# A vision tower on one core: one attention product moved by a group, and the row gathers of a linear-attention layer started in sixes

## The chip, the cores and the metric

The program runs on one core of a Trainium2 chip. The core has five engines with queues of their own: TensorE (PE) for matrix products, VectorE (DVE), ScalarE (ACT), GpSimd (POOL) and SyncE (SP), which issues most transfers. The metric is the device time of one execution in microseconds. Before the change it is 721.51 us, the median of three runs (718.78, 721.51 and 723.24).

## The reference

Everything is float32. The reference is a tokenizer for four images and two transformer layers. Tokens of one image are repeated three times, so the kernel computes 784 rows an image and writes each row out three times. The parts that the change touches are the first attention and the second one:

```python
# layer 0: attention between the images, one weight for a pair of images and a channel of a head
att = einsum('slhc,tlhc->sth', q, k) * scale     # sum over rows l and channels c
att = softmax(att, axis=1)
o = einsum('sth,tlhc->slhc', att, v) * g
...
# layer 0: a mixture of six experts, two for each row
combined = sum(sel * routing_weights[..., None], axis=2)
...
# layer 1: linear attention
q, k, v = split(layernorm(h) @ W_qkv + b_qkv, 3, axis=2)
q2 = _l2_normalize(q*q / (sum(q*q) + EPS_DIV), axis=-1)      # q and k have their means taken off
k2 = _l2_normalize(k*k / (sum(k*k) + EPS_DIV), axis=-2)
kv = einsum('bnc,bnd->bcd', k2, v)
attn = v + einsum('bnc,bcd->bnd', q2, kv) / sqrt(N)
h = h + attn @ W_out + b_out
```

In the first attention a "product" is one entry of `einsum('slhc,tlhc->sth')` before the sum over a head's channels: image s times image t, summed over the 784 rows, for one half of the 256 channels. In the mixture the two expert results of a row lie in HBM wherever the routing put them, so the second layer has to gather them row by row.

## The kernel before

**Layout.** The rows of the residual stream `h` are held in 25 tiles of 128 rows by 256 channels: six tiles an image, and one (`LT`) for the sixteen rows that each image has left over. The program is unrolled: every loop below is a Python loop that emits instructions.

**Front.** The tiles are worked in eight `groups` of three, the first with the left-over tile added. `keys_values(g)` takes the normalised, transposed rows of group g and computes its part of K and V on PE; ACT copies the results into `kT` and `vT`. In between it does three things for later groups: `second_norm(g + 2)`, the statistics of group g+2, which alternate between DVE (means and variances, reciprocals) and ACT (square roots); `turn_second(g + 1)`, transposes on PE and their ACT copies into `mT`, from which the next group's products are taken; and on DVE `second_rows(g + 2)`, and the addition of a bias to `h`. The order is written out by hand for PE, ACT and DVE, so an engine takes its instructions in exactly the order in which the code calls them.

After group 1 the queries of image 0 are computed. Then, after each odd group, DVE takes two products of image 0, one for each half `o` of the channels, with the image whose keys have just been finished: `products(0, o, [g // 2])`. Each is one DVE instruction over 128 x 784 elements, with its sum read out after it. The products with the last image follow behind the loop.

**Experts.** Rows are scattered to HBM by expert (`send`, one indirect DMA from POOL for each tile and choice), PE works the blocks, and results go back to `yrows` in HBM.

**Layer 1, linear attention.** The 24 full tiles are `units` 0 to 7 of three tiles each, and the left-over tile is unit 8 (`LU`). For one unit the steps are

- `fetch(u)`: for each of its three tiles and both choices one indirect DMA on POOL's queue that gathers 128 rows of 1 KB from `yrows` into the tile `ys`: six gathers for a unit, in the order (tile 0, choice 0), (tile 0, choice 1), (tile 1, choice 0) and so on. `ys` has three buffers, so unit u reuses the buffer of unit u-3 and waits until that was read.
- `stats_one(u, j)`: DVE adds the two gathered tiles to `h`, weighted, and takes mean and variance of tile j. These two additions (line 1760) are the only readers of `ys`.
- `norm_root(u)`, `norm_rows(u)` (together `normalise`): square root on ACT, then DVE writes the normalised rows to `xa`, one of four tiles used in turn (`xa_of(u)`).
- `x_t(u)`: transposes on PE, copied by ACT or DVE into `lxT`; `qk_mm`, `qk_add`, `qk_squares`: queries and keys; `scales(u)` and `fold(u)`: their norms.
- For each image b: `k_x_tiles`, `k_x_left` (the products of keys and rows, PE), `k_norm(b)` (PE sums the squared keys into `pn`, ACT takes the root into `kn`, DVE the reciprocal), `k_x_out` (DVE scales the products by `kn` into `g`), `g_t` (PE transposes `g`, ACT copies), `kv_out` (PE and DVE), and then `rows_out` for its two units.

The part up to `rows_out(1)` is written out by hand for PE, ACT, DVE and POOL. Behind it a loop `for u in range(4, LU + 2)` leaves the order to the scheduler of the framework. The calls of `fetch` stand in this order: units 0, 1, LU and 2 among the expert blocks; 3 and 4 one after the other behind the four POOL instructions that mask the left-over rows (`xaM`, line 2222); 5 and 6 later in the hand-written part; 7 at the top of the loop's first pass. Since POOL has nothing else to do there, its queue holds the thirty gathers of units 3 to 7 one after the other, held back only by the three buffers.

Of the kernel before, what the change touches and what calls it, by code (L numbers as in the profile page):

```python
# [21 lines left out]
F32 = mybir.dt.float32  # L22
# [50 lines left out]
def tile_vit_tower(ctx: ExitStack, tc: tile.TileContext, a: dict, out: bass.AP):  # L73
    nc = tc.nc
# [267 lines left out]
    groups = [list(range(g, g + 3)) for g in range(0, NT - 1, 3)]  # L342
# [1020 lines left out]
    with tc.manual_schedule(engines=by_hand):  # L1363
        last_rows(n - 2)
        turn_second(0)
        second_rows(1, second_norm(1))
        keys_values(0)
        for g in range(1, len(groups)):
            keys_values(g)

            if g == 1:
                for o in range(2):
                    q_mm(0, o)
                    q_copy(0, o)
            if g % 2 and g + 1 < len(groups):
                for o in range(2):
                    products(0, o, [g // 2])
    front.close()
# [196 lines left out]
    past, u, ua, ub = (s - 2, 0, TPI), (s - 1, 0, TPI), (s, 0, GT), (s, GT, TPI + 1 - GT)  # L1575
# [137 lines left out]
    LU = len(units)  # L1713
# [10 lines left out]
    def xa_of(u):  # L1724
        return xaL if u == LU else xas[u % 4]

    def own_of(pool, u, shape, tag, bufs):
        if u == LU:
            return pool.tile([shape[0], 1, *shape[2:]], F32, tag=f"{tag}L", name=tag, bufs=1)
        return pool.tile(shape, F32, tag=tag, name=tag, bufs=bufs)  # L1730

    xaM = lina.tile([TT, NI, D + 2], F32, tag="xaM", name="xaM", bufs=1)
    for xa in (*xas, xaL):
        nc.gpsimd.memset(xa[:, :, D : D + 2], 1.0)
    xTs, qTs, uks, qks, sums, gs, kvos, stats, ys = ({} for _ in range(9))

    def fetch(u):

        if u >= len(units):
            return  # L1740
        b, j0, n = units[u]
        y = ys[u] = own_of(lina, u, [TT, UT, 2, D], "ys", 3)
        for j in range(n):
            for k in range(2):
                t = b * TPI + j0 + j
                got = nc.gpsimd.indirect_dma_start(  # L1746
                    out=y[:, j, k, :], out_offset=None, in_=yrows[:, :],
                    in_offset=bass.IndirectOffsetOnAxis(ap=pos[:, k, t : t + 1], axis=0),
                )
                tc.add_to_no_dep_group("fetched", got.ins)  # L1750

    lw, behind = [], []
# [27 lines left out]
    def normalise(u):  # L1780
        norm_root(u)
        norm_rows(u)
# [10 lines left out]
    def norm_rows(u):  # L1793
        if u >= len(units):
            return
        b, j0, n = units[u]
        t0 = b * TPI + j0
        mv, r = stats.pop(u)
        nc.vector.reciprocal(r[:, :n], r[:, :n])
        xa = xa_of(u)  # L1800
        for j in range(n):
            nc.vector.tensor_scalar(
                xa[:, j, :D], h[:, t0 + j, :], mv[:, j, 0:1], r[:, j : j + 1],
                ALU.subtract, ALU.mult,
            )
        if len(pending) < 7:
            pending.append(u)
        else:
            residual(u)
# [248 lines left out]
    def scales(u):  # L2058
        root(u)
        factors(u)  # L2060
        k_rows(u)
        q_rows(u)
        return k_squares(u)
# [41 lines left out]
    def k_norm(b):  # L2105

        acc = sums.pop(b)
        pn = psum_s.tile([P, 512], F32, tag="pss", name="pn")
        for c in range(2):
            of_c = slice(c * P, (c + 1) * P)  # L2110
            nc.tensor.matmul(pn[:, c : c + 1], acc[:, of_c], ones[:TT], start=True, stop=False)
            nc.tensor.matmul(
                pn[:, c : c + 1], squares[LU][:, 0, of_c], ofimage[:, b : b + 1],
                start=False, stop=True,
            )
        kn = small.tile([P, 2], F32, tag="kn", name="kn")
        nc.scalar.activation(kn, pn[:, :2], AF.Sqrt, scale=float(REP), bias=zero)
        nc.vector.tensor_scalar(kn, kn, 1e-12, None, ALU.max)
        nc.vector.reciprocal(kn, kn)
        return kn  # L2120

    def k_x_out(b, kn):
        g = gs[b] = lin.tile([P, 2, D + 2], F32, tag="g", name="g")
        for c in range(2):
            nc.vector.tensor_scalar(
                g[:, c, :], pgxs.pop((b, c)), kn[:, c : c + 1], REP / math.sqrt(REP * SEQ),
                ALU.mult, ALU.mult,
            )
# [32 lines left out]
    def rows_out(u):  # L2161
        for done in rows_out_parts(u):
            pass
        return done
# [39 lines left out]
    with tc.manual_schedule(engines=by_hand | {ENG.Pool}):  # L2204
        x_t(1)
        for j in range(UT):
            qk_mm(0, j)
            qk_add(0, j)
            qk_squares(0, j)
        root(0)  # L2210
        for j in range(UT):
            qk_mm(1, j)
        qk_add(1, 0)
        qk_squares(1, 0)
        stats_one(LU, 0)
        norm_root(LU)
        factors(0)
        qk_add(1, 1)
        qk_squares(1, 1)
        norm_rows(LU)  # L2220
        for b in range(NI):
            nc.gpsimd.tensor_scalar(
                xaM[:, b, :], xaL[:, 0, : D + 2], ofimage[:, b : b + 1], None, ALU.mult
            )
        fetch(3)
        fetch(4)
        qk_add(1, 2)
        qk_squares(1, 2)
        root(1)
        q_rows(0)  # L2230
        stats_one(2, 0)
        next(steps)
        x_t(LU)
        q_t(0)
        k_rows(0)
        next(steps)
        stats_one(2, 1)
        factors(1)
        q_rows(1)
        k_rows(1)  # L2240
        qk_mm(LU, 0)
        stats_one(2, 2)
        norm_root(2)
        next(steps)
        Wvo, bvo = lw[:2]
        q_t(1)
        qk_add(LU, 0)
        qk_squares(LU, 0)
        root(LU)
        norm_rows(2)  # L2250
        fetch(5)
        squares[0] = k_squares(0)
        factors(LU)
        fold(0, squares.pop(0))
        k_rows(LU)
        squares[LU] = k_squares(LU)
        q_rows(LU)
        squares[1] = k_squares(1)
        fold(1, squares.pop(1))
        k_x_tiles(0)  # L2260
        x_t(2)
        k_x_left(0)
        kn = k_norm(0)
        k_x_out(0, kn)
        qk_mm(2, 0)
        qk_add(2, 0)
        qk_squares(2, 0)
        stats_one(3, 0)
        qk_mm(2, 1)
        qk_add(2, 1)  # L2270
        qk_squares(2, 1)
        q_t(LU)
        gT = g_t(0)
        stats_one(3, 1)
        qk_mm(2, 2)
        qk_add(2, 2)
        kv_out(0, gT)
        qk_squares(2, 2)
        stats_one(3, 2)
        normalise(3)  # L2280
        rows_out(0)
        x_t(3)
        root(2)
        factors(2)
        k_rows(2)
        q_rows(2)
        fetch(6)
        for j in range(2):
            qk_mm(3, j)
            qk_add(3, j)  # L2290
            qk_squares(3, j)
            stats_one(4, j)
        squares[2] = k_squares(2)
        qk_mm(3, 2)
        qk_add(3, 2)
        qk_squares(3, 2)
        stats_one(4, 2)
        root(3)
        norm_root(4)
        norm_rows(4)  # L2300
        parts_ = rows_out_parts(1)
        next(parts_)
        fold(2, squares.pop(2))
        factors(3)
        k_rows(3)
        q_t(2)
        x_t(4)
        for done in parts_:
            pass
        q_rows(3)  # L2310
        squares[3] = k_squares(3)
        fold(3, squares.pop(3))
        behind.append(done.ins.name)
    one_side[0] = False
    later = {5: (0, 1), 6: (2, 3), 7: (4, 5, 6)}
    for u in range(4, LU + 2):
        b, odd = divmod(u - 2, 2)
        one_image = not odd
        if u + 3 < LU:
            fetch(u + 3)  # L2320
        if u == LU:
            shared = shared1(0)
        if one_image:
            k_x(b)
            q_t(u - 1)
        if u < LU:
            q_k(u, 0, 2)
        if one_image:
            gT = g_t(b)
        if u < LU:  # L2330
            q_k(u, 2, UT)
            squares[u] = scales(u)
        if one_image:
            kv_out(b, gT)
        if u == LU - 1:
            rows_in(0)
            turn_rows(0)
            gate(0)
        if u < LU - 1:
            x_t(u + 1)  # L2340
        done = rows_out(u - 2)
        for k in later.get(u, ()):
            residual(pending[k], done.ins.name)
        if u == LU + 1:
            rows_left()
        if u < LU:
            fold(u, squares.pop(u))
            if u % 2:
                q_t(u - 1)
# [103 lines left out]
```

## Time and profile before

| what | us |
|---|---|
| median of three runs | 721.51 |
| the profiled execution's own time | 743.29 |
| its span, first to last instruction | 741.6 |
| PE busy in the span | 692.4 |
| DVE busy | 459.2 |
| ACT busy | 331.7 |
| POOL busy | 127.2 |

The profiled execution is 21.8 us longer than the median. Its stages, from the view that cuts the span into windows:

| stage (us from the start) | length | PE busy | POOL busy | granted PE clock |
|---|---|---|---|---|
| tokenizer, 0 to 130 | 130 | 120.27 | 18.77 | 1.00 |
| keys, values, attention, 130 to 207 | 77 | 73.20 | 0.00 | 0.98 |
| attention and the row scatters, 207 to 303 | 96 | 84.12 | 54.81 | 0.93 |
| experts, 303 to 434 | 131 | 128.69 | 12.79 | 1.00 |
| linear attention begins, 434 to 462 | 28 | 24.84 | 17.85 | 1.00 |
| 462 to 480 | 18 | 7.67 | 11.42 | 0.83 |
| linear attention, 480 to 600 | 120 | 117.67 | 11.52 | 0.98 |
| last mixture, 600 to 742 | 142 | 135.98 | 0.00 | 0.99 |

A line of the timeline reads: start, busy time, engine, line of the code, operation, out<-in, shapes, and how many instructions are merged into it. In square brackets stands how long the engine was idle before it and what released it. "issue" means that the profile shows no wait, and "remote" or "another core or an unknown queue" that it found no event near enough to name. The end of a PE instruction is modelled, not observed.

### The profile page before, as it was taken

The numbers are of one execution on the slowest core, as the hardware profiler recorded it, in microseconds if no ns is written. First come the engines' busy times: TensorE is split into PE (matmuls) and PEld (weight loads), VectorE is DVE, ScalarE is ACT, GpSimd is POOL, SyncE is SP. The second block draws the span as 40 slices with busy tenths as digits, with TensorE's granted clock in tenths as the row PEclk, the third lists the DMA queues.
The fourth block names the chain that finished last, engine by engine and source line by source line (L and its number), as shares of the span: only waits on it lengthen the run. The fifth ranks groups of instructions, "written<-read, shape, count | busy, mean of one in ns | idle before, by whom it ended". The sixth has DMA issues, their size and how long they took to land.

```text
span 741.6 us, 9843 instructions
## 1 busy us (share of the span) xinstructions
PE 692.4 (93%) x3043; PEld 477.3 (64%) x3043; DVE 459.2 (62%) x1385; ACT 331.7 (45%) x816; POOL 127.2 (17%) x238
## 2 busy tenths in 40 slices
PE   7899999899998897999999998499999999999996
PEld 4556655566655686788888856267776855555553
DVE  6476865769988643357555668179978653444441
ACT  1565674556797652223322337154645232222221
POOL 6300000000065356200002328533000000000000
PEclk9999999999999898999999999799999999999999
DMA  6999997000036834222334432211000013321333
GB/s 192 334 426 425 426 425 300 0 1 0 1 121 193 290 103 140 92 86 93 94 114 128 147 97 79 85 43 42 2 1 1 4 29 118 108 87 52 121 106 100
DMA packets 56476, 96.49 MB, mean 130 GB/s; under 512 B 6696, under 2 KB 46350, under 8 KB 56424
## 3 DMA queue, kind: packets, MB, share of 16 engines
q1 hardware_dynamic: 49924, 79.69, 30.1%
q0 software_dynamic: 5600, 14.32, 6.3%
q10 hardware_dynamic: 900, 1.86, 0.8%
q8 instruction: 24, 0.39, 0.2%
q14 instruction: 28, 0.23, 0.1%
HBM read 30.75 MB, written 65.09 MB: 129 GB/s over the span
## 4 chain that ended last, share of the span: by engine, by line
PE 55%; DVE 5%; ACT 2%; another core or an unknown queue 2%; issue 1%; DMA 1%; SPq 0%; DVEq 0%; ACTq 0%
PE pb L1539 13%; PE pe L320 6%; PE pyb L1557 6%; PE ps L320 5%; PE pqk L1994 4%; PE ps L2403 3%; PE pout L2173 3%; PE pout L2178 3%; PE pukx L2093 2%; PE pt L311 2%; PE pe L2373 2%; PE ps L2397 2%; PE ptb L1524 1%; PE pkvo L2153 1%
## 5 line engine op out<-in xcount | busy, mean ns | idle before, releaser
L1154 POOL DMA_INDIRECT xrows<-xn,pos x50 | 54.2, 1084 | 217.9 <-DVE nm L1010 178.3
L1746 POOL DMA_INDIRECT ys<-yrows,pos x50 | 49.2, 984 | 151.4 <-DMA yrows<-yb 120.0
L1545 ACT ACTIVATE hb<-pb,own 128x256 f32<-128x256 f32 (+1 forms) x74 | 33.5, 457 | 57.2 <-PE pb L1539 33.1
L1539 PE MATMUL pb<-xTb,own 128*128 128x256 f32 (+1 forms) x240 | 53.3, 364 | 4.8 <-ACT xTb L1528 2.6
L1539 PE MATMUL pb<-hb,own 128*128 128x256 f32 (+1 forms) x240 | 54.6, 368 | 0.3 <-DVE hb L1547 0.2
L1557 PE MATMUL pyb<-own,hb 128*128 128x256 f32 x216 | 53.5, 388 | 0.3 <-ACT hb L1545 0.2
L1994 PE MATMUL pqk<-Wqkv,lxT 128*128 128x512 f32 x100 | 47.7, 624 | 3.4 <-issue 3.2
L1539 PEld LDWEIGHTS pb<-xTb,own 128*128 128x128 f32 x240 | 42.1, 191 | 10.6 <-ACT xTb L1528 3.2
L320 PE MATMUL pe<-xT,eW 128*128 128x512 f32 (+1 forms) x112 | 46.0, 553 | 0.0
L1557 PEld LDWEIGHTS pyb<-own,hb 128*128 128x128 f32 x216 | 41.1, 195 | 6.8 <-ACT hb L1545 1.1
L1539 PEld LDWEIGHTS pb<-hb,own 128*128 128x128 f32 x240 | 41.9, 195 | 5.1 <-DVE hb L1547 0.9
L1563 DVE TENSOR_TENSOR yb<-pyb,eb 128x512 f32<-128x512 f32 (+1 forms) x30 | 19.1, 638 | 37.7 <-PE pyb L1557 32.8
L637 PE MATMUL pw<-Wall,pT 128*128 128x512 f32 (+1 forms) x96 | 42.4, 592 | 0.0
L1528 ACT COPY xTb<-ptb 128x512 f32<-128x512 f32 (+1 forms) x30 | 16.3, 542 | 54.4 <-PE ptb L1524 46.2
L907 DVE SCALAR_TENSOR_TENSOR prod<-kq 128x784 f32<-128x784 f32 x32 | 30.6, 970 | 13.2 <-issue 5.9
L1994 PEld LDWEIGHTS pqk<-Wqkv,lxT 128*128 128x128 f32 x100 | 19.4, 202 | 24.0 <-issue 22.1
L320 PEld LDWEIGHTS pe<-xT,eW 128*128 128x128 f32 x112 | 20.2, 190 | 21.6 <-issue 16.5
L1515 DVE COPY own<-kq 128x1540 f32 x30 | 29.1, 974 | 6.6 <-ACT xTb L1528 3.1
L311 PEld LDWEIGHTS pt<-ident,xn 128*128 128x128 f32 x200 | 24.3, 145 | 12.7 <-issue 10.0
L1547 DVE TENSOR_SCALAR hb<-pb,own 128x256 f32<-128x256 f32 (+1 forms) x46 | 20.3, 445 | 17.9 <-PE pb L1539 17.4
L637 PEld LDWEIGHTS pw<-Wall,pT 128*128 128x128 f32 (+1 forms) x96 | 17.9, 189 | 20.5 <-issue 18.5
L311 PE MATMUL pt<-ident,xn 128*128 128x128 f32 x200 | 29.0, 284 | 1.8 <-issue 1.6
(418 smaller groups left out, 1439.7 us busy)
## 6 DMA issues: line engine op xcount, KB each, us to landing
xrows<-nothing SPq DMA_DIRECT2D x22, 896.0 KB
yrows<-nothing SPq DMA_DIRECT2D x22, 896.0 KB
out_dram<-h SPq DMA_DIRECT2D x23, 384.0 KB
xb<-xrows SPq DMA_DIRECT2D x24, 256.0 KB
yrows<-yb SPq DMA_DIRECT2D x24, 256.0 KB
kq<-in_L_ffn_expert_w_dram SPq DMA_DIRECT2D x18, 256.0 KB
wb<-wd SPq DMA_DIRECT2D x16, 128.0 KB
img<-in_x_dram SPq DMA_DIRECT2D x5, 294.0 KB
```

Source lines behind the costliest of these rows:

```text
L311: nc.tensor.transpose(pt[:, j * TT : (j + 1) * TT], xn[:, j, c * P : (c + 1) * P], ident[:TT, :TT])
L320: nc.tensor.matmul(pm[: wcols.stop - wcols.start, :n], w[:, c, wcols], xT(c), start=(c == 0), stop=(c == chunks - 1),)
L637: nc.tensor.matmul(pm, pixels(c, tiles[j]), Wall[: K1[c], c, :], start=(c == 0), stop=(c == 1))
L907: nc.vector.scalar_tensor_tensor(prod, qTs[s][:, o, :], 1.0, kT[:, o, t * SEQ : (t + 1) * SEQ], ALU.mult, ALU.mult, accum_out=atts[s][:, o ...
L1154: put = nc.gpsimd.indirect_dma_start(out=xrows[:, :], out_offset=bass.IndirectOffsetOnAxis(ap=pos[:, k, t0 + j : t0 + j + 1], axis=0), in_ ...
L1515: nc.vector.tensor_copy(w, ewf[0][:, bass.ds(off, EW)])
L1539: nc.tensor.matmul(pm, wm[:, c, o * P : (o + 1) * P], src[:, c, :], start=(c == 0), stop=(c == 1),)
L1545: nc.scalar.activation(dst[:, o, :], pm, AF.Relu, bias=b)
L1557: nc.tensor.matmul(pm[:, t, :], src[:, c, t * P : (t + 1) * P], wm[:, c, :], start=(c == 0), stop=(c == 1),)
L1746: got = nc.gpsimd.indirect_dma_start(out=y[:, j, k, :], out_offset=None, in_=yrows[:, :], in_offset=bass.IndirectOffsetOnAxis(ap=pos[:, k, ...
L1994: nc.tensor.matmul(pqk, xTs[u][:, c, cut(j, 1)], Wqkv[:, c, : 2 * D], start=(c == 0), stop=(c == 1),)
L2173: nc.tensor.matmul(pm[:, i, :], xT[:, c, cut(j, 1)], Wvo[:, c, :], start=(c == 0), stop=False,)
```

## The change

In the front, the product of image 0 with itself for the second half of the channels is taken after group 2 instead of after group 1. The later products stay: the third branch catches groups 3 and 5 as before.

In the linear attention, `fetch` gets a second argument, one element of a tile. When it is given, POOL first copies that element into a new one-element tile `paused`; the gathers are called after it. The fetches are moved in the code: unit 4's from behind `xaM` to behind the reciprocal of image 0's norm (`kn`), unit 5's to behind unit 3's normalised rows, unit 6's to behind unit 4's, and unit 7's to the end of the loop's first pass, with an element of unit 5's rows.

```diff
@@ the front
-            if g % 2 and g + 1 < len(groups):
+            if g == 1:
+                products(0, 0, [0])
+            elif g == 2:
+                products(0, 1, [0])
+            elif g % 2 and g + 1 < len(groups):
                 for o in range(2):
                     products(0, o, [g // 2])
@@ the tiles of the linear attention
     xaM = lina.tile([TT, NI, D + 2], F32, tag="xaM", name="xaM", bufs=1)
+    paused = lina.tile([1, 1], F32, tag="paused", name="paused", bufs=1)
...
-    def fetch(u):
+    def fetch(u, behind=None):
 
         if u >= len(units):
             return
         b, j0, n = units[u]
+        if behind is not None:
+            nc.gpsimd.tensor_copy(paused, behind)
         y = ys[u] = own_of(lina, u, [TT, UT, 2, D], "ys", 3)
@@ the part written out by hand
         fetch(3)
-        fetch(4)
         qk_add(1, 2)
...
         norm_rows(2)
-        fetch(5)
         squares[0] = k_squares(0)
...
         k_x_left(0)
         kn = k_norm(0)
+        fetch(4, kn[:1, :1])
         k_x_out(0, kn)
...
         normalise(3)
+        fetch(5, xa_of(3)[:1, 0, :1])
         rows_out(0)
...
         q_rows(2)
-        fetch(6)
...
         norm_rows(4)
+        fetch(6, xa_of(4)[:1, 0, :1])
         parts_ = rows_out_parts(1)
@@ the loop
     for u in range(4, LU + 2):
         b, odd = divmod(u - 2, 2)
         one_image = not odd
-        if u + 3 < LU:
-            fetch(u + 3)
...
         if u < LU:
             q_k(u, 2, UT)
             squares[u] = scales(u)
+            if u + 3 < LU:
+                fetch(u + 3, xa_of(u + 1)[:1, 0, :1])
```

Built, the two kernels have the same instructions in the same order on PE, ACT and SP. DVE's order differs by the one product. POOL's queue behind `xaM` is, before, thirty gathers; after, six gathers, the copy of `kn`, six gathers, the copy of unit 3's element, six gathers, the copy of unit 4's element, twelve gathers, the copy of unit 5's element.

## The prediction, made before the changed kernel ran

> **What bounds the kernel now.** I read the page first, then the windows by stage, the chain of waits in order of time, and the timelines of single engines around each moved instruction.
>
> ```profile
> span 741.6 us, 9843 instructions
> PE   7899999899998897999999998499999999999996
> PE 55%; DVE 5%; ACT 2%; another core or an unknown queue 2%; issue 1%; DMA 1%; SPq 0%; DVEq 0%; ACTq 0%
> ```
>
> PE is the bound nearly everywhere. One slice in forty stands out, with 4 tenths. The windows place it: between 462 and 480 us PE is busy 7.67 of 18 us, while POOL issues gathers without a pause. The chain of waits, in order of time, has two pieces there that belong to no engine:
>
> ```profile
> 460.99 1.34 ACT sq L2055 x4
> 462.33 4.61 another core or an unknown queue
> 466.97 0.48 ACT lxT L94
> 467.44 0.95 issue
> 468.39 0.48 ACT lxT L94
> 468.87 10.05 another core or an unknown queue
> 478.95 0.27 ACT kn L2117
> ```
>
> The timelines of PE, ACT, DVE and POOL say who waits for whom:
>
> ```profile
> 463.98 0.36 PE L2112 MATMUL pn<-ofimage,sq 128*128 128x1 f32 x2
> ...
> 478.95 0.26 ACT L2117 ACTIVATE kn<-pn,zero 128x2 f32<-128x2 f32 x1 [10.07 <-remote]
> ...
> 479.24 0.17 DVE L2118 TENSOR_SCALAR kn<-kn 128x2 f32<-128x2 f32 x1 [16.01 <-ACT kn L2117]
> ...
> 475.83 0.94 POOL L1746 DMA_INDIRECT ys<-yrows,pos  x1 [0.30 <-issue]
> ```
>
> ACT's root needs only `pn`, whose last matmul stands at 463.98, with a modelled end of 464.34. It starts 14.6 us later, 2.2 us after the last of eighteen gathers issued without a wait (454.14 to 476.77). DVE waits for that root and PE for DVE. The waits show a smaller case in the row scatters, POOL's other indirect DMAs:
>
> ```profile
> DVE sel L1144 <- remote: 6.9, 1, 6.9
> ACT hb L1545 <- remote: 5.3, 1, 5.3
> ```
>
> There `pcount` ends at 274.93 by its model and DVE takes it at 281.02, 1.1 us after a run of twelve scatters (264.63 to 279.89). So in this execution PE's results arrive late when POOL has issued many indirect DMAs in a row. I call it the hold-up; its price here is 478.95 less the 464.5 at which `kn` could have run, 14.4 us.
>
> **The change part by part.**
>
> *The product.* In front of group 2's statistics ACT and PE wait:
>
> ```profile
> 143.97 0.30 ACT L286 ACTIVATE rstd<-mv,eps 128x3 f32<-128x3 f32 x1 [1.18 <-DVE mv L284]
> 145.81 2.85 PE L320 MATMUL pkv<-mT,Wk 128*128 128x384 f32 x8 [0.30 <-ACT mT L1317]
> ```
>
> One product is 0.89 us from start to start (140.45, 141.35, 142.24). Without the second one DVE's statistics begin at 141.35 and ACT's root 0.89 us sooner, inside its wait of 1.18. PE gets back at most its 0.30. Behind group 2's addition, which now ends 0.89 earlier, the product takes the 0.89 again, so group 3's statistics start at 147.56 as before. ACT's next root (149.28) has no wait in front, its copies `mT` run from 150.42 to 151.63, and PE wants the second of them at about 151.8 even when 0.3 sooner. The product's result is first read at 162.71. Sum: -0.3 us; bounds 0 and -0.3 (with a gain of 0.89 excluded by PE's own wait).
>
> *The gathers.* Nothing is removed: thirty gathers stay, 0.95 us each and 0.30 between, 1.25 apart; six take 7.5. From the start of a gather to the landing of its rows is 2.5 to 2.8 us (501.86 to 504.4, 508.18 to 511.0). POOL's queue holds nothing else behind them, and SP's is not touched. Every fetch is on the path only if its first reader on DVE has to wait:
> - Unit 4 starts after `kn` (reciprocal ends at 479.61): rows from 482.4, all by 488.7; DVE wants them at 496.26, 498.42 and 500.59. Slack over 11 us.
> - Unit 5 starts after the first row of unit 3 (ends 490.66): rows from 493.4 to 499.7; wanted from 507.50 to 512.41. Slack over 11.
> - Unit 6 starts after the first row of unit 4 (ends 503.26): rows from 506.0, every 1.25 us to 512.3; the readers stand at 511.27, 512.89, 515.32, 516.59, 518.86, 520.31. Slack 5.2 at the least.
> - Unit 7 has no pause: its copy stands behind its gathers in POOL's queue, since the loop is left to the scheduler and nothing ties them. It follows unit 6 at 510.9: rows from 513.5; wanted at 519.34, 522.79 and from 527.80. Slack 5.8.
>
> All four slacks lie behind `kn`, so they stay if the hold-up before it goes. Cost 0; the cover is those microseconds, and what is late beyond them is paid one for one, as the weighted additions stand in DVE's order ahead of `kn` of image 1 (512.33), for which PE waits.
>
> *Four copies of one element on POOL.* No such row is in the trace; the nearest are POOL's memsets of one column, 0.10 us, and its 128x258 rows, 1.02. I take 0.2 each; either end fits into 5.2. A gain is excluded for work that is added.
>
> *Waits.* DVE's rows of unit 7 and ACT's root of image 3 now name POOL, whose copies were done some 40 us and more before: 0. The table load ahead of that last root now waits for PE's `pn`. It ran at 577.20, when `pn` was just done, and DVE used `kn` only at 583.05, 3.6 us after it was ready (579.49). Cost 0, the cover 3.6.
>
> *The hold-up.* With the change POOL stops at 461.5 until `kn` is there, so in an execution like this one `pn` would come at about 463.6 to 464.5 and 13 to 14.4 us go. A new hold-up may come from the twelve gathers of units 6 and 7 (503.4 to 518.5): the twelve scatters cost 6.1.
>
> Does the timed kernel pay the hold-up at all? The timed median is 21.8 us below this execution. PE is idle 49.6 us in the windows of all stages, and its instructions run at one rate wherever it is fed (0.43 us for 512 columns), so the 21.8 must come out of idle time or a lower clock. If the 14.4 stayed, the other 39 us, mostly the first transfers (9.7), the tail (6.0) and short dependencies, would have to give 21.8. If it goes, and with it the late results beside the scatters (2.7 us of PE before 281.28, 1.9 before 294.90, some colder clock), the sum is about 20. So I take the hold-up as belonging mostly to the profiled execution: -0.3 for the timed kernel, not -14.
>
> Two rules of the Trainium skill bear on this. The rows say PE's results are 14.4 us late beside gathers. "SBUF — State Buffer", section Who interferes with whom, says a DMA never contends with a compute engine and only VectorE and GpSimd share a port: by it spacing the gathers is worth nothing, 721.2; by the row alone, 707. "NOTIFIC — the notification-queue block", section 7.1, says that the recorder's internal pipeline holds its producers back rather than lose a record. No row here shows that, but it would reconcile the two and agrees with the idle-time count.
>
> Sums: the profiled execution, 743.29 - 0.3 - 13 or so, plus 0 to 6: 730 to 736. The timed one, 721.51 - 0.3 = 721.2.
>
> **The rivals.**
> - *The hold-up is real in timed runs.* For: it is in the rows, and twice beside POOL. Against: the idle-time count. Then 721.5 - 13.2 + 0 to 6 gives 708 to 714.
> - *The hold-up moves onto the twelve gathers, slower than before.* Before, units 6 and 7 were two sixes with a pause of 5.4 us (496.48 to 501.86); after, they are twelve in a row beside `k_x(1)`, where PE has no idle time to lose. If timed runs feel this and not the place at 464, the price is 6.1 as for the twelve scatters, and about 1.7 for PE's colder clock afterwards (four matmuls at 0.85 instead of 0.43 us from 467.50): 721.2 + 7.8 = 729. It decides once unit 6's and 7's gathers hold up PE by more than their surroundings absorb. Against: the sixes now there (489.26, 501.86) held nothing up on the chain.
> - *The change doesn't do what it says.* It is so for unit 7, whose rows aren't paused. If POOL's copies held nothing else either, 721.2 as well.
>
> **How the numbers follow.** About 1% (7.2 us: 714.3 and 728.7) is what a measurement of this kernel tells from no change. Likeliest, 0.81: nothing on the path but -0.3, 721.2, between 718 and 725 as the three runs spread. Hold-up real: 0.14, 708 to 714.3 in 0.12 of it. Moved onto the twelve: 0.04. Rows late by more than 5.2 us for another reason: 0.01. So faster 0.12, within 1% 0.83, slower 0.05. The range, 711 to 725, leaves out the lower half of the fast case (0.07), the slow ones (0.05) and the likeliest's tails (0.06).
>
> **What would show it.** Right: POOL's gathers in runs of 6, 6, 6 and 12 behind `xaM`; no unnamed 10 us before `kn`; a span near 730 beside a timed median within 3 us of before; PE's 0.30 before 145.81 gone. Wrong: a timed median under 714; DVE waiting for `ys` at an addition of unit 6 or 7; an unnamed wait between 489 and 506 in the new times, where the twelve run.

## The result, and the profile after

The changed kernel takes 717.06 us, the median of eleven runs (715.16 to 719.26). The kernel before takes 721.51 in as many (718.78 to 723.7). The ratio is 0.994, with a 95% interval of 0.9924 to 0.9956: 4.45 us less, a small gain. The interval is clear of 1, though the slowest runs of the one kernel and the fastest of the other overlap (718.78 to 719.26). The prediction said 721.2 us and "within 1%". The second holds; the size does not. It had the change at -0.3 us, and some 4 us came from a place that it had not costed.

The profiled execution of the kernel after is the first surprise. It took 716.3 us, as long as an ordinary run, so recording a profile does not by itself lengthen the kernel. The page of the kernel after, its head, the row of PE's busy tenths and the shares of the chain that ended last:

```profile
span 714.6 us, 9849 instructions
...
PE   7899999999998899999999998999999999999996
...
PE 58%; DVE 3%; ACT 2%; issue 1%; DMA 1%; DVEq 0%; ACTq 0%; SPq 0%
```

The slice with 4 tenths is gone, and with it the share of "another core or an unknown queue". By the prediction's own figure, 14.4 us, that is about half of the 27.0 between the two profiled executions (741.6 and 714.6), but between the timed medians there are only 4.45 us. The experiments show that these are two different things.

The 4.45 us were won at 120 to 132 us. There DVE takes the two products of image 0 with itself. DVE's timeline of the kernel before (start, busy time, engine and line, operation, shapes; in brackets the idle time in front and its releaser):

```profile
120.57 0.98 DVE L907 SCALAR_TENSOR_TENSOR prod<-kq 128x784 f32<-128x784 f32 x1 [1.00 <-ACT kq L882]
...
127.44 0.98 DVE L907 SCALAR_TENSOR_TENSOR prod<-kq 128x784 f32<-128x784 f32 x1 [5.89 <-issue]
...
128.34 0.42 DVE L283 BATCH_NORM_STATS2 st<-h 128x6 f32<-128x256 f32 x1
```

The second product's last operand is a copy by ACT, as ACT's timeline of the kernel before shows (`kq` is the tile of the keys and queries):

```profile
122.68 0.49 ACT L882 COPY kq<-pq 128x392 f32<-128x392 f32 x1 [0.83 <-PE pq L320]
```

It ends at 123.17. Of the 5.89 us that DVE stands idle, the first 1.6 belong to it; for the other 4.3 the product has its operands and still does not start. "issue" only says that the timeline found no releaser near enough. The next statistics stand behind the product in DVE's queue. In the same kernel before, ACT's timeline and PE's show who waits for those statistics:

```profile
130.07 0.30 ACT L286 ACTIVATE rstd<-mv,eps 128x3 f32<-128x3 f32 x1 [4.33 <-DVE mv L284]
```

```profile
131.91 4.54 PE L320 MATMUL pkv<-mT,Wk 128*128 128x384 f32 x8 [3.45 <-ACT mT L1317]
```

The chain is product, statistics, root, `mT` (which stands behind the root in ACT's queue), PE. After the change, DVE's timeline reads:

```profile
120.61 0.97 DVE L907 SCALAR_TENSOR_TENSOR prod<-kq 128x784 f32<-128x784 f32 x1 [1.00 <-ACT kq L882]
...
121.51 0.42 DVE L283 BATCH_NORM_STATS2 st<-h 128x6 f32<-128x256 f32 x1
...
129.20 0.96 DVE L907 SCALAR_TENSOR_TENSOR prod<-kq 128x784 f32<-128x784 f32 x1
```

The statistics begin 6.83 us sooner (121.51 for 128.34), and the product itself, at 129.20, has no bracket: whatever it waited for is over by then. ACT's root stands at 125.68 without a wait, and PE's idle piece is gone. PE's timeline of the kernel after:

```profile
128.34 2.74 PE L320 MATMUL pkv<-mT,Wk 128*128 128x384 f32 x8
```

What did it wait for? `prod` has two buffers in the pool `attm`. The second one lies in part on the space of `nothing`, the tile of zeros that is the source of the transfers that fill `xrows` and `yrows`. Those 46 transfers follow one another every 2.2 us, and their traffic ends between 126 and 127 us. The first product writes buffer one; the second writes buffer two and must not begin before the zeros have been read out: as built, it waits for the semaphores of those transfers besides that of ACT. The first profile does hold the answer, in another view: asked for the tile `nothing`, it lists under "who waited for it" the row `DVE prod L907: 5.9, 1`. This theory is called P below. Its rivals are that the gathers' spacing gave the time, or that the hold-up of the prediction is paid in timed runs (theory H).

### The profile page after: what moved, and what is told of

Read it like the earlier page. It is cut to its first block, busy times and chain, and to the rows that moved or that the text cites. A ratio compares the mean times of both kernels' runs of the same rounds, so it can differ in the third digit from the quotient of the medians.

```text
span 714.6 us, 9849 instructions
## 1 busy us (share of the span) xinstructions
PE 684.8 (96%) x3043; PEld 474.3 (66%) x3043; DVE 458.9 (64%) x1385; ACT 332.0 (46%) x816; POOL 129.3 (18%) x242
## 4 chain that ended last, share of the span: by engine, by line
PE 58%; DVE 3%; ACT 2%; issue 1%; DMA 1%; DVEq 0%; ACTq 0%; SPq 0%
PE pb L1543 12%; PE pe L320 6%; PE pyb L1561 6%; PE ps L320 5%; PE pqk L2001 5%; PE ps L2410 3%; PE pukx L2100 3%; PE pout L2180 3%; PE pout L2185 3%; PE pt L311 2%; PE pe L2380 2%; PE ps L2404 2%; PE ptb L1528 2%; PE pkvo L2160 1%; PE ps L2402 1%
## 5 line engine op out<-in xcount | busy, mean ns | idle before, releaser
L1543 PE MATMUL pb<-hb,own 128*128 128x256 f32 (+1 forms) x240 | 53.0, 360 | 0.3 <-DVE hb L1551 0.2
L2001 PE MATMUL pqk<-Wqkv,lxT 128*128 128x512 f32 x100 | 44.9, 594 | 0.2 <-ACT lxT L94 0.2
L907 DVE SCALAR_TENSOR_TENSOR prod<-kq 128x784 f32<-128x784 f32 x32 | 30.6, 969 | 7.3 <-ACT kq L882 3.9
L2015 ACT ACTIVATE qk<-qk 128x256 f32<-128x256 f32 x50 | 20.4, 408 | 22.9 <-DVE qk L2007 20.8
```

Source lines behind the costliest of these rows:

```text
L907: nc.vector.scalar_tensor_tensor(prod, qTs[s][:, o, :], 1.0, kT[:, o, t * SEQ : (t + 1) * SEQ], ALU.mult, ALU.mult, accum_out=atts[s][:, o ...
L1543: nc.tensor.matmul(pm, wm[:, c, o * P : (o + 1) * P], src[:, c, :], start=(c == 0), stop=(c == 1),)
L2001: nc.tensor.matmul(pqk, xTs[u][:, c, cut(j, 1)], Wqkv[:, c, : 2 * D], start=(c == 0), stop=(c == 1),)
```

## The experiments

**The kernel before, once more (e0).**

> The kernel before, unchanged, profiled a second time. Theory P (the gain is the moved product, whose second buffer waits for the transfers that fill HBM with zeros): the second product of image 0 starts near 127.4 us again with some 5.9 us of DVE idle before it, and PE has about 3.4 us of idle time before the next keys, near 131.9. Theory H (the gain is the late results of PE beside the gathers): an unnamed wait of several us stands in front of the root of image 0's key norm again, and the span is well over 720. If the late results belong to that one profiled execution alone, the wait is gone here and the span is near 720.

It took 719.22 us, with a span of 717.5 (741.6 in the first profile). The view of windows, one row for each kernel, 462 to 480 us (length, then busy time and instructions of PE, weight loads, DVE, ACT and POOL, then granted clock, DMA share, GB/s); first the first profile of before, then e0:

```profile
462.00:480.00 18.00, 7.67 (x26) 4.04 (x24) 1.65 (x6) 1.55 (x5) 11.42 (x12) 0.83 0.33 95
```

```profile
462.00:480.00 18.00, 17.51 (x74) 12.61 (x73) 13.87 (x38) 8.77 (x34) 10.80 (x12) 1.00 0.28 84
```

POOL has twelve instructions in both, and PE is busy for 17.51 us of 18 in the second. The 14.4 us hold-up belonged to that one execution. No wait is put down to "remote" any more. The product's wait is there again, at 127.19 after 4.84 us of idle time. Here the view names `kq` of line 1342 as releaser, a copy of a later group's keys that this product does not read; a named releaser is only the event that stands nearest. The view of `nothing` lists no waiter this time. PE's timeline of e0:

```profile
131.66 2.85 PE L320 MATMUL pkv<-mT,Wk 128*128 128x384 f32 x8 [2.39 <-ACT mT L1317]
```

**The product alone (e1).** The gathers stay as they were.

```diff
-            if g % 2 and g + 1 < len(groups):
+            if g == 1:
+                products(0, 0, [0])
+            elif g == 2:
+                products(0, 1, [0])
+            elif g % 2 and g + 1 < len(groups):
```

> The product of image 0 with itself, second half of the channels, behind group 2; the gathers as before. Theory P: a ratio near 0.994, about 4.4 us less, nearly the whole gain of the change; DVE takes group 3's statistics near 121.5 us and the product near 129.2 without a wait. Theory H: at most the 0.3 us that the prediction gave it, a ratio of 0.9996 or above.

716.24 us (715.34 to 718.63), ratio to before 0.9942 [0.9922, 0.9963]. The whole gain is here. The product stands at 129.46 without a wait, and DVE's statistics stand in front of it:

```profile
121.78 0.42 DVE L283 BATCH_NORM_STATS2 st<-h 128x6 f32<-128x256 f32 x1
```

**The gathers alone (e2).** The kernel after, with the three branches of the front put back to the one of before.

```diff
-            if g == 1:
-                products(0, 0, [0])
-            elif g == 2:
-                products(0, 1, [0])
-            elif g % 2 and g + 1 < len(groups):
+            if g % 2 and g + 1 < len(groups):
```

> The gathers in rows of six with their pauses; the products as before. Theory P: a ratio of 1.000, within 0.002 of it, since every gather lands at least 5 us before it is read, and the wait of 5.9 us before the second product is there. Theory H: a ratio near 0.994, and no late result of PE before the root of image 0's norm.

721.84 us (718.79 to 724.85), ratio 1.0011 [0.9996, 1.0026]: worth nothing. The wait is in place (5.08 us before 128.30), and PE's timeline of e2 adds something:

```profile
132.77 4.24 PE L320 MATMUL pkv<-mT,Wk 128*128 128x384 f32 x8 [2.64 <-ACT mT L1317]
```

The same eight matmuls take 2.85 us in e0, after 2.39 us of idle time. Here they are at a colder clock, which the windows of e2 around that place show (granted clock in the third column from the end):

```profile
126.50:132.50 6.00, 3.63 (x16) 2.04 (x14) 3.26 (x13) 1.42 (x4) 0.00 (x0) 0.98 0.02 7
132.50:138.50 6.00, 5.73 (x18) 3.53 (x19) 4.00 (x14) 2.82 (x8) 0.00 (x0) 0.74 0.00 0
```

So an idle piece of 2.64 us costs 2.64 + (4.24 - 2.85) = 4.0 us. That is close to the 4.45 of the medians. In e0 the clock stayed at 1.00 behind 2.39 us of idle time, and that execution, at 719.22, is one of the shorter ones of before. Single executions differ by as much elsewhere too: the first product, ahead of which these kernels do not differ, begins at 120.54 in e3 and at 122.24 in e2. So a gain of this size is read from the medians, and a profile serves to say where it lies.

**One buffer for the product (e3).** The kernel before with nothing moved; `prod` has no second buffer that could lie on the zeros.

```diff
-            prod = attm.tile([P, SEQ], F32, tag="prod", name="prod")
+            prod = attm.tile([P, SEQ], F32, tag="prod", name="prod", bufs=1)
```

> The kernel before with one buffer for the products' scratch tile instead of two, and nothing moved: the second product writes where the first one did and no longer where the source of the zero transfers lay. Theory P: the wait for the transfers goes, so about 4 us less, a ratio of 0.994 to 0.995, slightly less gain than the moved product since the product still stands in front of group 3's statistics (0.89 us, inside ACT's or PE's time). Theory H: 1.000. If the gain came from having less DVE work in front of group 3's statistics and not from the transfers, also about 1.000.

716.36 us (715.55 to 718.84), ratio 0.9938 [0.9922, 0.9955]. The second product stands behind 1.65 us in place of 4.84 to 5.89, and what is left is an operand that it does need:

```profile
123.17 0.97 DVE L907 SCALAR_TENSOR_TENSOR prod<-kq 128x784 f32<-128x784 f32 x1 [1.65 <-ACT kq L882]
```

The order of the work was not what mattered; the buffer was. One argument brings what the move brings. The intervals of e1, e3 and the kernel after cover each other, so none of them can be called the fastest.

**Two more transfers of zeros, in the kernel before (d1) and after (d2).** If P holds, the wait must grow with them.

```diff
-    for r in range(0, XROWS, 7 * P):
+    for r in [*range(0, XROWS, 7 * P), 0]:
```

> The kernel before, with two more zero-filling transfers of 896 KB (46 become 48; the first rows of xrows and yrows are filled twice). The zero transfers follow one another every 2.2 us, so the last lands about 4.4 us later, near 131 us. If the second product of image 0 waits for them (its second buffer lies over their source) and DVE's statistics, ACT's root and PE stand behind it: the product begins at about 131.5 instead of 127.2 to 128.3, PE's idle time before it takes up the next group grows from about 2.5 to about 7 us, and the time is 4.0 to 4.6 us more, about 725.5, ratio 1.006. If the gain of the product's move had another cause (only the 0.89 us of one product ahead of the statistics): the same time as before, 721.2, ratio 1.000.

726.1 us (725.83 to 727.97), ratio 1.0088 [1.0061, 1.0115]: 4.9 us more by the medians (721.18 for before) and 4.4 to 8.3 by the interval, for an expected 4.0 to 4.6. This time the wait is long enough for the profile to name it. DVE's timeline, then PE's, of d1:

```profile
132.14 0.98 DVE L907 SCALAR_TENSOR_TENSOR prod<-kq 128x784 f32<-128x784 f32 x1 [8.56 <-DMA yrows<-nothing]
```

```profile
136.61 4.42 PE L320 MATMUL pkv<-mT,Wk 128*128 128x384 f32 x8 [6.11 <-ACT mT L1317]
```

> The kernel after, with the same two extra zero transfers. Here the product stands at 129.20 without a wait, so 2.2 to 2.5 of the 4.4 us are left to it. Behind it in DVE's queue are the next statistics, ACT's root (131.81), and behind that root in ACT's queue the copies mT, which PE wants at 134.16. Waiting theory: the product begins at about 131.6, PE gets an idle piece of about 2 us, the time is 1.5 to 2.4 us above the kernel after, about 719, ratio to before 0.997. If the product's wait is not the cause: as the kernel after, 717, ratio 0.994.

719.87 us (718.59 to 722.84), ratio to before 0.9989 [0.9977, 1.0001], 2.8 us above the kernel after, for an expected 1.5 to 2.4. The product now waits for the zeros in its new place too. DVE's timeline, then PE's, of d2:

```profile
133.20 0.98 DVE L907 SCALAR_TENSOR_TENSOR prod<-kq 128x784 f32<-128x784 f32 x1 [2.69 <-DMA yrows<-nothing]
```

```profile
137.67 4.54 PE L320 MATMUL pkv<-mT,Wk 128*128 128x384 f32 x8 [2.11 <-ACT mT L1317]
```

PE loses 2.11 us, and the eight matmuls behind it take 4.54 for 2.85: 3.8 us in this execution, a little above the 2.8 of the median. The move escapes the wait only because the zeros are done in time: the two transfers add some 4.4 us and the product waits for 2.69 of them, so the margin is about 1.7. P stands on both sides: with the wait taken away without a move (e3), and with the wait made longer (d1, d2).

**How late may unit 6's rows be (s1 to s4)?** The prediction costed the gathers at nothing by a slack of 5.2 us for unit 6. The first two experiments put POOL work between the pause and unit 6's gathers in the kernel after: three memsets in s1, eight in s2.

```diff
-        fetch(6, xa_of(4)[:1, 0, :1])
+        nc.gpsimd.tensor_copy(paused, xa_of(4)[:1, 0, :1])
+        for _ in range(3):
+            nc.gpsimd.memset(idle, 0.0)
+        fetch(6)
```

> The kernel after, with three POOL memsets of a scratch tile (128x1600) between the pause and the gathers of unit 6: about 4.3 us of delay for the gathers of units 6 and 7. In the profile after, unit 6's rows would land from 479.6 on every 1.25 us, and its readers stand at 485.35, 485.83, 488.26 and later, so the least slack is 4.9 us. Slack theory: nothing changes, 717, ratio to before 0.994, no DVE wait for ys. If the gathers' spacing had been what gave the time (their start close to the reader's need): some microseconds more.

718.24 us (716.93 to 720.24), ratio to before 0.9964 [0.9952, 0.9976]: 1.2 us above the kernel after, with no wait for `ys`. The two intervals just touch, so the 1.2 is likely and not certain. The delay is not what cost it. DVE's and PE's timelines of s1:

```profile
476.76 2.30 DVE L1810 TENSOR_SCALAR xa<-h,mv,rstd 128x256 f32<-128x256 f32 x3
```

```profile
479.11 0.66 PE L311 MATMUL pt<-ident,xa 128*128 128x128 f32 x4 [1.24 <-DVE xa L1810]
```

The three rows of `xa` take 1.06 us in the kernel after. Beside the memset that begins at 477.49 they take 2.30, and PE waits for them.

> The kernel after, with eight such memsets, about 11.5 us of delay. Slack theory, paid one for one beyond 4.9 us: DVE waits for ys about 6.5 us at an addition of unit 6, before the reciprocal of image 1's kn, for which PE waits: 6 to 7 us more than the kernel after, about 723.5, ratio to before 1.003. If DVE's order absorbs lateness beyond the slack: less than 2 us more, ratio below 0.997.

724.05 us (723.05 to 725.31), ratio 1.0055 [1.0038, 1.0073]. The time fits the expectation of 723.5, but not for its reason: DVE has no wait for `ys`. The scheduler of the loop, which sees the longer POOL queue when it orders the program, had put DVE's additions later and moved some instructions of PE and ACT as well, and the memsets stretched DVE again: `xa` 2.30 for 1.06, three rows of `qk` 4.71 for 0.87. PE waits 1.23 and 3.65 us behind these, and from 489 to 495 its granted clock is 0.72. So s1 measured the memsets and s2 the memsets and another order, not the lateness. The other two delay unit 6 with transfers only, gathers into a scratch tile: three in s3, nine in s4.

```diff
...
+        for _ in range(extra):
+            t = b * TPI + j0
+            nc.gpsimd.indirect_dma_start(
+                out=idle, out_offset=None, in_=yrows[:, :],
+                in_offset=bass.IndirectOffsetOnAxis(ap=pos[:, 0, t : t + 1], axis=0),
+            )
...
+        fetch(6, extra=3)
```

> The kernel after, with three extra gathers of 128 rows into a scratch tile ahead of unit 6's own, in place of the memsets: 3 x 1.25 = 3.75 us of delay[...]. The order on PE, DVE and ACT is that of the kernel after. Slack theory (4.9 us): no wait for ys, 717, ratio to before 0.994; the 1.2 us that the three memsets cost should be gone, since DVE's rows xa were stretched beside them (2.30 us for 1.06). If the delay itself had cost the 1.2 us: 718.2, ratio 0.996.

719.26 us (718.42 to 721.7), ratio 0.9975 [0.9957, 0.9992]. The expected delay of 3.75 us was wrong: all three write the same tile, so each waits for the one before to land. POOL's timeline of s3:

```profile
479.30 0.22 POOL L2314 COPY paused<-xa 1x1 f32<-1x1 f32 x1 [4.60 <-DVE xa L1816]
479.98 0.97 POOL L1753 DMA_INDIRECT idle<-yrows,pos  x1 [0.46 <-issue]
483.01 1.05 POOL L1753 DMA_INDIRECT idle<-yrows,pos  x1 [2.06 <-DMA idle<-yrows,pos]
486.11 0.94 POOL L1753 DMA_INDIRECT idle<-yrows,pos  x1 [2.05 <-DMA idle<-yrows,pos]
487.36 0.94 POOL L1760 DMA_INDIRECT ys<-yrows,pos  x1 [0.30 <-issue]
```

Unit 6's first gather starts 8.06 us behind the copy, where it is 0.68 in the kernel after: 7.4 us late. DVE's timeline of s3 shows what is not covered:

```profile
490.09 0.48 DVE L1774 SCALAR_TENSOR_TENSOR h<-ys,wk,h 128x256 f32<-128x256 f32 x1 [2.82 <-DMA ys<-yrows,pos]
```

7.4 less 2.82 is a slack of 4.6 us, for the predicted 5.2. PE then has two idle pieces of 1.12 us that the kernel after does not have, together 2.24, and the median is 2.2 us above that of the kernel after. In this case the lateness beyond the slack is paid nearly one for one. The order on PE, DVE and ACT is that of the kernel after, as it is in s1, and `xa` was not stretched here, so this is the clean one of the four. PE's timeline of s3:

```profile
496.70 1.99 PE L2167 MATMUL pkvo<-Wvo,gT 128*128 128x256 f32 x8 [1.12 <-ACT gT L2158]
...
519.47 0.38 PE L2125 MATMUL pn<-ones,acc 128*128 128x1 f32 x2 [1.12 <-DVE acc L2088]
```

> The kernel after, with nine such gathers, 11.3 us of delay, of which 6.4 lie beyond the slack. As built, the scheduler of the loop puts DVE's additions of units 6 and 7 later in its order. If lateness is paid one for one all the same: 6 us or more above the kernel after, 723.5, ratio 1.003. If the later place of the additions takes it up, and the memsets' stretching of DVE was most of what the eight memsets cost (4.71 for 0.87 us, and 2.30 for 1.06): 1 to 3 us, 718 to 720, ratio 0.996 to 0.999.

729.68 us (729.3 to 730.08), ratio 1.0114 [1.0091, 1.0137]. For the same reason the delay is 25.8 us (501.59 less 475.09 and 0.68) and not 11.3, so neither expectation applies as it was written. PE's timeline of s4:

```profile
516.26 0.66 PE L311 MATMUL pt<-ident,xa 128*128 128x128 f32 x2 [12.18 <-DVE xa L1816]
```

12.2 us of PE's time and 12.6 in the median are paid of 25.8. The other 13 are slack and the other order that the scheduler gave the program, on DVE, PE and ACT; how much is which was not told apart.

## Why the prediction was right or wrong

**The product: wrong place, and with it the only term that moved the time.** The step costed it "in front of group 2's statistics", with the pair of products at 140.45 and 141.35, and found that "PE gets back at most its 0.30". That pair is the one after group 3 (`g // 2` is 1), which the change does not touch. The product that moves is the second after group 1, at 127.44. There DVE was idle for 5.89 us, ACT for 4.33 and PE for 3.45. All three stood in the profile of before. The list of DVE's waits had it in one row (waited for, us in total, times, longest):

```profile
DVE prod L907 <- issue: 5.9, 1, 5.9
```

The prediction quoted two rows of that kind and passed this one over, and it nowhere asks what the place that the product writes to has to wait for. The term should have been about -4: PE's idle piece of 2.4 to 3.5 us and up to 1.7 for the colder clock behind it. Measured alone (e1) it is 0.58% of 721.2, 4.2 us (2.7 to 5.6 by the interval; 5.0 between the medians), and 4.45 between the medians of the whole change. "bounds 0 and -0.3" were no bounds, because they bounded another instruction. That "within 1%" held all the same is luck in part: the term that was missed is smaller than the 7.2 us of that range.

**The gathers: right.** Alone they are 1.0011 [0.9996, 1.0026]. POOL's runs behind `xaM` were 6, 6, 6 and 12, as predicted, and unit 7's copy stands behind its gathers (492.16), so it pauses nothing. The copies took 0.18 to 0.23 us, for 0.2. Unit 6's slack was 4.6 for 5.2.

**The hold-up: right for the timed kernel.** The step said that it belongs "mostly to the profiled execution". It belongs to that one execution: the four later profiles with the same eighteen gathers in a row (e0, e1, e3, d1) have none, and neither have those with the twelve (the kernel after, e2, d2). The idle-time count led to the right answer. The reconciliation by the recorder was not supported: these later executions were recorded too and took the ordinary time. What made PE's results late that once stays open. The forecast of 730 to 736 for the profiled execution after, which kept part of it, missed: 716.3. Of the Trainium skill's two rules weighed there, "SBUF — State Buffer", section Who interferes with whom, gave 721.2 against 707 by the row alone, and e2's 721.84 agrees with the page. "NOTIFIC — the notification-queue block", section 7.1, describes a holding back of producers that no later profile shows.

**The rivals.** The hold-up in timed runs (708 to 714) and its move onto the twelve gathers (729) did not happen. In the kernel after, the twelve gathers run from 476.93 to 492.16, and PE has no idle piece there. That the change does not do what it says holds for unit 7 only.

**The signs named beforehand.** "PE's 0.30 before 145.81 gone" was a sign at the wrong place. "a timed median within 3 us of before" failed by 1.45 us, and that was the sign that something had been left out. The prediction took 1% for what a measurement tells from no change; the interval of this one is 0.16% to either side, so a change of 0.6% could be told.

## What to carry to other kernels

When a profile has an idle piece ended by "issue", or by an event that the instruction does not need, in front of an instruction that has all its operands, ask what its output buffer overlays, and ask the view of that tile who waited for it: in a pool, a second buffer can lie on the source of a transfer that is still being read, and everything behind that instruction in its queue waits too. Before costing a moved instruction, find it in the trace by loop index and count, not by its name alone, since here three pairs of one name stood within 40 us. A stall in one profiled execution that is longer than the gap to the timed median is to be profiled again before a theory is built on it.

## What the runs showed of the hardware

- An idle piece of 2.1 to 3.5 us in PE can cost more than its length: the mean clock granted in the 6 us behind it was 0.72 to 0.74 (before, e2, d2), with 0.50 in the whole microseconds from 133 to 135 (before) and 139 to 141 (d2), and eight matmuls took 4.24 to 4.54 us for 2.85. It is not so in each execution: behind 2.39 us the clock stayed at 1.00 (e0), behind 2.11 it fell (d2).
- A POOL memset stretches some DVE instructions beside it: a TENSOR_SCALAR from SBUF to SBUF took 2.30 us for 1.06 and 4.71 for 0.87, and seemed to last until a memset was over, while TENSOR_TENSOR instructions in the same stretch took what they take without it, one that reads PSUM (`h<-pout`, 0.67 for 0.68) and one that does not (`acc<-sq`, 0.41 for 0.41).
- Gathers into one tile, each waiting for the one before to land, run 3.0 to 3.1 us apart (s3), and 1.25 apart into different places.
- One profiled execution out of five with the gathers in before's order (before, e0, e1, e3, d1) showed PE's results up to 14.4 us late; its cause is not known.
